# Block 3 of a two-layer kernel: half 0 run three weights ahead of half 1 at the end, with step lists of its own, and the residual behind the steps

## The chip, the core and the metric

The kernel runs on one core of a Trainium2 chip. The metric is the time of one execution in device microseconds, as the median of several runs; less is better.

## The reference

Two layers act on x, of shape (4, 256, 512), in float32. Each has a mixer and a feed-forward part, each behind a layer norm and added to x:

```python
x = x + _L0_attn_ref(_layernorm(x), ...)   # block 1: gated linear attention, 32 heads, chunks of 128
x = x + _L0_ffn_ref(_layernorm(x), ...)    # block 2: router, 8 of 64 expert biases
x = x + _L1_attn_ref(_layernorm(x), ...)   # block 3: state space mixer, 128 heads of 64, 8 groups
x = x + _L1_ffn_ref(_layernorm(x), ...)    # block 4: 16 of 64 rank-16 adapters
```

Block 3 projects x to a gate, to x/B/C (which go through a causal convolution of four taps and a silu) and to time steps; within chunks of 128 positions it multiplies by decays exp(difference of cumulated steps); the result is gated by silu(gate), normalised over each of the 8 groups of 1024 channels, and projected back to 512:

```python
Y = (Y_diag + Y_off).reshape(b, s, H, P) + hs * D[None, None, :, None]
g = y * jax.nn.silu(gate)
gg = g.reshape(b, s, G, INTER // G)
gg = gg * jax.lax.rsqrt(jnp.mean(gg * gg, axis=-1, keepdims=True) + EPS)
return jnp.einsum('bsi,oi->bso', gg.reshape(b, s, INTER) * norm_w, out_proj_w)
```

Block 4 takes the 16 largest of 64 scores per row, their softmax as gates, and adds the gated low-rank products.

## The kernel before

The 1024 rows are two halves of 512 (half 0 and half 1), each of four tiles of 128 rows. x stays in SBUF. Every large projection is done in float32 accuracy by three matmuls of split operands (high times high, high times low, low times high), so one projection of 128 channels (`proj`, L197) is 12 matmuls of 128x512.

Weights come in blocks of 512 KB through the class `Weights`: a DMA from SP's queue into one of two raw buffers (L167), a cast to the high part on ACT (L135), a subtraction for the low part on POOL (L138).

Block 3 (`state_space`) goes over pairs of channel chunks. A pair (g, cp, half) is two chunks of 128 channels of group g (0 to 7), cp from 0 to 3, for one half; it needs three weights: wx (input), wg (gate), wo (output). Its steps, each a letter in a step list:

- I0, I1 (`inputs`): 12 matmuls ps_x; the convolution as one ACT pass and three DVE passes (`conv`, L709); a silu on ACT. G0, G1 (`gate`): 12 matmuls ps_g, silu on ACT.
- X0, X1 (`sums`): a DMA gb of broadcast cumulated steps (L283), their differences on DVE and POOL (m, L290), a causal mask on POOL (L292). D0, D1 (`decays`): exp on ACT (each change between silu and exp is a table load, L1112), then DVE's product with the group's matrix (m, L750).
- T0, T1 (`turn`): transposes, then xd and xe on DVE (L774, L783). M0, M1 (`mixer`): 12 small matmuls ps_y; xs on DVE (L807) and its gate product on POOL (L811); yh on ACT, yl on DVE (L816); a square on ACT whose sum sqs is kept on POOL (L825).
- O0 to O3 (`output`): for each row tile six matmuls ps_o (L851, two PSUM buffers) that DVE adds to acc (L857). In the last pair of a group (cp = 3) step O0 first makes r, the inverse root of the mean square (`scale`: 8 PE records ps_m, one DVE, one POOL instruction, L837), and each O adds its tile to x with `x += acc * r` (L860, the residual).
- B is the group's B and C, W starts one more weight, and P and E take one step of the side work in `k.side` (E also where that step needs an exp table).

One round of the loop in `run` has three pairs: O of `before`, T and M of `p`, all else of `after`. The order of pairs is written out: the first four weights run half 0 and then half 1; then each weight runs both halves in turn; the last `LONE3` weights run half 0 and then half 1 again, and each half loads its own weights. With `LONE3 = 2` the pairs end with

    (7,1,0) (7,1,1) | (7,2,0) (7,3,0) (7,2,1) (7,3,1)

A half that has all its groups goes to `done(half)`, which puts block 4's preparation of that half into `k.side`: statistics (L83), rstd on POOL (L87, L88), xn (L96), transposes, xs_hi and xs_lo (L121, L122), the logits (ps_lg), the 16 largest on DVE, the gates through DRAM and, for half 0, 96 matmuls ps_h (`first`). `adapters.run` then does the rest: hid of half 0, half 1's preparation, 96 output matmuls of half 0 (ps_o, L1077), 96 matmuls ps_h and 96 output matmuls of half 1. The low parts of its weights (wa, wb) are POOL subtractions too.

The step lists are program order. The framework's scheduler then moves instructions of each engine by its own estimate of readiness, so the built order, not the list, is what an engine runs; each engine runs its instructions strictly in that order.

Of the kernel before, what the change touches and what calls it, by code (L numbers as in the profile page):

```python
# [18 lines left out]
P = 128  # L19
# [3 lines left out]
HT = NT // 2  # L23
# [1 line left out]
EPS = 1e-5  # L25
GONE = -30000.0
YB = 3
LONE1, FIRST3, LONE3 = 3, 1, 2
PUMP = 1
AHEAD = 0  # L30
BANK1, BANK3 = "o", "x"
# [1 line left out]
STEP1 = "K S0 W T S1 S2 W G0 G1 K C K P U A0 K W P A1 T P P Q0 N0 W W N1 Q1 T T W K D F".split()  # L33
SIDE1 = "S0 W G0 T P K C W W P P W S1 K G1 S2 U P A0 N0 A1 P Q0 T W T F W N1 K Q1 T T D W W".split()
STEP3 = "W T0 T1 B I0 W M0 M1 X0 X1 I1 O0 G0 W W O1 W W P O2 W W G1 P W O3 D0 D1 W W".split()
FILL3 = "B X0 X1 I0 I1 P P G0 G1 W W P P W D0 D1 E E".split()
SIDE3 = "T0 T1 I0 I1 M0 M1 P B X0 X1 P P O0 W O1 G0 G1 W W P O2 O3 W P W P D0 D1 E E".split()

# [610 lines left out]
def state_space(k, tc, io):  # L649
# [4 lines left out]
    NC = 8  # L654
# [60 lines left out]
    def group(p):  # L715

        g, half = p.g, p.half
        bc = [
            k.wk.tile([P, FREE], F32, tag="y", name=f"bc_{g}_{half}_{n}", bufs=4) for n in range(2)
        ]  # L720
        for n, first in enumerate((BS, CS)):
            conv(proj(k, tc, chunk(p.w.bc(), n), half, f"bc_{g}_{half}_{n}"), bc[n], first + g)
        s = own.only.tile([P, 3, 2, P], F32, tag="cb", name=f"cb_{g}_{half}", bufs=2)
        for b in range(2):
            ps = k.psum.tile([P, 3, P], F32, tag="x", name=f"ps_cb_{g}_{half}_{b}")
            for n, (zs, zl) in enumerate(((0, 0), (1, 1), (0, 1))):
                fs, fl = (2 * b + zs) * P, (2 * b + zl) * P
                nc.tensor.matmul(
                    ps[:, n, :], bc[0][:, fs:fs + P], bc[1][:, fl:fl + P],
                    start=True, stop=True,  # L730
                )
            own.copied = nc.scalar.copy(s[:, :, b, :], ps)
        cbs[g, half] = s

    def sums(p, n):
        hs = slice(2 * (p.ch + n), 2 * (p.ch + n) + 2)
        p.e[n] = exponents(
            k, tc, cum[p.half][:, hs, :], start[p.half][:, :, hs], f"{p.name}_{n}", 2
        )

    def decays(p, n):


        m, across = p.e.pop(n)
        exps = k.act(m[:, 2], across, AF.Exp), k.act(m[:, 0:2], m[:, 0:2], AF.Exp)
        if p is pairs[0]:
            for one in exps:
                k.behind(one, own.copied, "C.B first")
        mh = m.rearrange("p z (h b) l -> p z h (b l)", h=2)
        made = nc.vector.tensor_tensor(  # L750
            mh, mh, cbs[p.g, p.half].rearrange("p z b l -> p z (b l)").unsqueeze(2)
            .to_broadcast([P, 3, 2, 2 * P]), ALU.mult,
        )
        p.m.append(m)
        p.due.append(made)

    def inputs(p, n):
        xs = k.wk.tile([P, FREE], F32, tag="a", name=f"xs_{p.name}_{n}", bufs=4)
        conv(proj(k, tc, chunk(p.w.x(), n), p.half, f"x_{p.name}_{n}"), xs, p.ch + n)
        p.xs.append(xs)  # L760

    def gate(p, n):
        sg = k.wk.tile([P, FREE], F32, tag="sg", name=f"sg_{p.name}_{n}", bufs=4)
        k.act(sg, proj(k, tc, chunk(p.w.g(), n), p.half, f"g_{p.name}_{n}", "g"), AF.Silu)
        p.sg.append(sg)

    def turn(p, n):

        nm, ch, xs = f"{p.name}_{n}", p.ch + n, p.xs[n]
        ps = k.psum.tile([P, HT, P], F32, tag="y", name=f"ps_t_{nm}")  # L770
        for t in range(HT):
            nc.tensor.transpose(ps[:, t, :], xs[:, t * P:t * P + P], k.ident)
        xd = k.wk.tile([P, HT, 2, D], F32, tag="xd", name=f"xd_{nm}")
        made = nc.vector.tensor_tensor(  # L774
            xd, ps.rearrange("p t (h d) -> p t h d", h=2),
            dt[p.half][:, :, 2 * ch:2 * ch + 2].unsqueeze(3)
            .to_broadcast([P, HT, 2, D]), ALU.mult,
        )
        p.xd.append(xd)
        p.due.append(made)  # L780
        if n == 0:
            p.xe = k.wk.tile([P, 2, 2, 2, D], F32, tag="xn", name=f"xe_{p.name}", bufs=1)
        made = nc.vector.tensor_tensor(  # L783
            p.xe[:, n], ps.rearrange("p (b z) (h d) -> p b z h d", b=2, h=2)[:, :, 0],
            start[p.half][:, 2, 2 * ch:2 * ch + 2, :].rearrange("p h b -> p b h").unsqueeze(3)
            .to_broadcast([P, 2, 2, D]), ALU.mult,
        )
        p.due.append(made)
# [38 lines left out]
    def scale(p):  # L827

        ps = k.psum.tile([P, HT], F32, tag="y", name=f"ps_m3_{p.name}")
        for t in range(HT):  # L830
            nc.tensor.matmul(
                ps[:, t:t + 1], sqs[p.g, p.half][:, t * P:t * P + P], k.ones,
                start=True, stop=True,
            )
        p.r = k.small([P, HT], f"r3_{p.name}", "r")
        nc.vector.tensor_scalar(p.r, ps, 1.0 / (NC * P), EPS, ALU.mult, ALU.add)
        nc.gpsimd.tensor_tensor(p.r, p.r, k.neghalf, ALU.pow)  # L837

    def output(p, t):
        if p.cp == 0 and t == 0:  # L840
            acc[p.g, p.half] = k.wk.tile([P, HT, HID], F32, tag="big", name=f"acc_{p.name}")
        if p.cp == NC // 2 - 1 and t == 0:
            scale(p)
        ps = k.psum.tile([P, HID], F32, tag="o", name=f"ps_o3_{p.name}_{t}")
        at = slice(t * P, t * P + P)
        i = 0
        for n in range(2):
            yh, yl = p.y[n]
            wh, wl = p.w.o()
            for y, w in ((yh, wh), (yh, wl), (yl, wh)):  # L850
                nc.tensor.matmul(ps, y[:, at], w[:, n, :], start=(i == 0), stop=(i == 5))  # L851
                i += 1
        a = acc[p.g, p.half][:, t, :]
        if p.cp == 0:
            nc.scalar.copy(a, ps)
        else:
            nc.vector.tensor_tensor(a, a, ps, ALU.add)  # L857
        if p.cp == NC // 2 - 1:
            xt = k.x[HT * p.half + t]
            nc.vector.scalar_tensor_tensor(xt, a, p.r[:, t:t + 1], xt, ALU.mult, ALU.add)  # L860

    cbs, sqs, acc = {}, {}, {}

    pairs, uses = [], []
# [4 lines left out]
    for together in order:  # L869
        pair = [(*divmod(n, NC // 2), half) for half in range(2) for n in together]  # L870
        for g, cp, half in pair:
            p = Ctx()
# [16 lines left out]
    def run(done):  # L889


        with tc.tile_pool(name="s3", bufs=1, reuse_waits="tile") as own.only:
            for i in range(-1, len(pairs) + 1):
                k.bank = BANK3 if i >= 0 else "o"
                before, p, after = (
                    pairs[j] if 0 <= j < len(pairs) else None for j in (i - 1, i, i + 1)
                )
                if i + 2 < len(pairs):
                    k.weights.due = pairs[i + 2].w.g.n
                else:  # L900
                    k.weights.due = len(k.weights.all) - 1
                if after is not None and after.half not in ready:
                    k.pump(1000, True)

                def shared():
                    if after.cp == 0:
                        group(after)

                def put(t):
                    output(before, t)  # L910
                    if t == HT - 1 and all(one.half != before.half for one in pairs[i:]):
                        done(before.half)

                step = dict(
                    B=shared, I=lambda n: inputs(after, n), G=lambda n: gate(after, n),
                    X=lambda n: sums(after, n), D=lambda n: decays(after, n), T=lambda n: turn(p, n), M=lambda n: mixer(p, n),
                    O=put, W=k.weights.step, P=k.pump, E=lambda: k.pump(1, True),
                )
                for one in FILL3 if i < 0 else SIDE3 if k.side else STEP3:
                    who = {"T": p, "M": p, "O": before, "P": k, "E": k, "W": k}.get(one[0], after)  # L920
                    if who is not None and (i >= 0 or not AHEAD or one[0] not in "IG"):
                        step[one[0]](*(int(n) for n in one[1:]))

    def ahead(i):

        p = pairs[0]
        assert 0 in ready
        n = i % 2
        if i < 2:
            inputs(p, n)  # L930
        elif i < 4:
            gate(p, n)
        else:
            sums(p, n)
# [315 lines left out]
```

## Time and profile before

| what | value |
|---|---|
| median of 3 runs (lowest, highest) | 2555.05 us (2549.81, 2555.57) |
| profiled execution: time; span | 2553.7 us; 2551.9 us |
| mean granted TensorE clock | 0.987 |
| PE, DVE, ACT, POOL busy | 96%, 80%, 57%, 62% of the span |
| first ps_g of pair (7,1,1) | 2301.1 us |
| table loads ahead of the exps of (7,1,0), (7,1,1), (7,2,0), (7,3,0), (7,2,1) | 2308.34, 2328.06, 2346.46, 2366.81, 2388.30 us |
| first matmul of half 1's last output tile | 2542.2 us |

PE is TensorE, DVE VectorE, ACT ScalarE, POOL GpSimd, SP SyncE. Times are microseconds from the start of the span. A number such as L857 is a line of the kernel before. Busy time is the time in which an engine had an instruction at work; a matmul of 128x512 lasts about 0.39 and the next starts 0.227 after it. "[6.61 <-DVE acc L857]" means that the engine was idle for 6.61 before this instruction, and that DVE's instruction on line 857 ended that.

### The profile page before, as it was taken

The page shows a single profiled execution, that of the slowest core. Times are in us where ns is not written, and L with a number is a line of the kernel's source. Part 1 is how long each engine was busy: PE and PEld are TensorE (multiplying, and loading weights), DVE is VectorE, ACT ScalarE, POOL GpSimd, SP SyncE. Part 2 cuts the span into 40 slices and gives each one's busy share as a digit, 9 for nine tenths or more (in the row PEclk, how much of TensorE's full clock was granted, in tenths as well). Part 3 has the DMA queues.
Part 4 walks back from the last instruction along what each step waited for, and adds up shares of the span by engine and source line. Part 5 has one row for each costly group of instructions (what it writes and reads, how often), then busy time and mean ns, then how long its engine had stood idle before and what let it go on. Part 6 is the DMA issues. An engine that isn't in the chain of part 4 may idle for free.

```text
span 2551.9 us, 36913 instructions
## 1 busy us (share of the span) xinstructions
PE 2438.3 (96%) x14000; PEld 2012.3 (79%) x14000; DVE 2037.0 (80%) x2629; ACT 1453.8 (57%) x2363; POOL 1584.7 (62%) x1123
## 2 busy tenths in 40 slices
PE   7999999999999998899999999999999999999899
PEld 6788787888877876678878888888888888887677
DVE  6776676767777878697998988988988988979873
ACT  3554454545554555475765756666757657657631
POOL 4655445556575646586774875856756865857840
PEclk9999999999999998999999999999999999999999
DMA  3321212212221322242322323322323223323321
GB/s 107 85 71 48 54 44 63 70 58 83 83 91 56 97 73 85 73 128 73 97 91 67 97 78 88 92 70 91 99 68 100 84 67 96 100 62 108 93 77 68
DMA packets 82896, 206.25 MB, mean 81 GB/s; under 512 B 8672, under 2 KB 10592, under 8 KB 82720
## 3 DMA queue, kind: packets, MB, share of 16 engines
q1 hardware_dynamic: 82720, 203.90, 26.6%
q8 instruction: 111, 1.82, 0.3%
q14 instruction: 65, 0.53, 0.1%
HBM read 200.86 MB, written 3.01 MB: 80 GB/s over the span
## 4 chain that ended last, share of the span: by engine, by line
PE 59%; DVE 17%; POOL 10%; ACT 6%; issue 5%; DMA 2%; SPq 0%; POOLq 0%; ACTq 0%; DVEq 0%
PE ps_g L197 12%; PE ps_x L197 8%; PE ps_o L851 8%; PE ps_o L452 5%; PE ps_q L197 5%; DVE m L750 4%; PE ps_y L797 4%; DVE conv L709 3%; PE ps_bc L197 3%; PE ps_sc L396 2%; PE ps_y L408 2%; POOL m L290 2%; ACT L1112 2%; POOL xs L811 2%; DVE yl L816 2%
## 5 line engine op out<-in xcount | busy, mean ns | idle before, releaser
L197 PE MATMUL ps_g<-xs_hi,wg_h 128*128 128x512 f32 x768 | 305.7, 398 | 5.3 <-ACT wg_h L135 2.4
L750 DVE TENSOR_TENSOR m<-m,cb 128x1536 f32<-128x1536 f32 x128 | 274.1, 2145 | 41.3 <-ACT m L1115 40.2
L197 PE MATMUL ps_g<-xs_lo,wg_h 128*128 128x512 f32 x768 | 300.9, 392 | 0.0
L197 PE MATMUL ps_g<-xs_hi,wg_l 128*128 128x512 f32 x768 | 299.6, 393 | 0.0
L709 DVE SCALAR_TENSOR_TENSOR conv<-ps_x,cw,conv 128x510 f32<-128x510 f32 (+2 forms) x384 | 269.9, 736 | 21.9 <-ACT conv L707 19.1
L1112 ACT ACT_TABLE_LOAD x191 | 245.1, 1283 | 3.8 <-PEq L1238 0.8
L851 PE MATMUL ps_o<-wo_h,yh 128*128 128x512 f32 x512 | 212.5, 415 | 19.4 <-DVE acc L857 18.6
L290 POOL TENSOR_TENSOR m<-gb,start 128x512 f32<-128x512 f32 x128 | 150.5, 1178 | 127.6 <-PE ps_y L797 82.1
L811 POOL TENSOR_TENSOR xs<-xs,sg 128x512 f32<-128x512 f32 x128 | 207.8, 1624 | 29.4 <-DVE xs L807 28.5
L825 POOL TENSOR_TENSOR sqs<-sqs,sq 128x512 f32<-128x512 f32 x112 | 193.3, 1726 | 34.6 <-ACT sq L823 34.2
L138 POOL TENSOR_TENSOR wo_l<-raw_wo,wo_h 128x1024 fp32r<-128x1024 f32 x60 | 148.1, 2468 | 93.2 <-ACT wo_h L135 87.4
L851 PE MATMUL ps_o<-wo_h,yl 128*128 128x512 f32 x512 | 199.3, 403 | 5.9 <-DVE yl L816 5.9
L197 PE MATMUL ps_x<-xs_lo,wx_h 128*128 128x512 f32 x512 | 203.0, 396 | 0.0
L851 PE MATMUL ps_o<-wo_l,yh 128*128 128x512 f32 x512 | 202.7, 396 | 0.0
L197 PE MATMUL ps_x<-xs_hi,wx_h 128*128 128x512 f32 x512 | 202.4, 395 | 0.0
L197 PE MATMUL ps_x<-xs_hi,wx_l 128*128 128x512 f32 x512 | 201.6, 394 | 0.0
L292 POOL TENSOR_SCALAR_AFFINE_SELECT m<-m 128x1024 f32<-128x1024 f32 x160 | 200.5, 1253 | 0.1
L1115 ACT ACTIVATE xs<-conv,cb 128x512 f32<-128x512 f32 x128 | 90.8, 723 | 191.5 <-DVE conv L709 191.5
L138 POOL TENSOR_TENSOR wx_l<-raw_wx,wx_h 128x1024 fp32r<-128x1024 f32 x38 | 96.1, 2529 | 159.8 <-ACT wx_h L135 147.1
L797 PE MATMUL ps_y<-m,xd 128*64 128x128 f32 x2048 | 177.7, 279 | 10.9 <-DVE m L750 8.1
L1115 ACT ACTIVATE m<-m 128x1024 f32<-128x1024 f32 (+1 forms) x160 | 181.6, 1135 | 9.1 <-POOL m L292 8.8
L138 POOL TENSOR_TENSOR wg_l<-raw_wg,wg_h 128x1024 fp32r<-128x1024 f32 x60 | 152.4, 2540 | 50.7 <-ACT wg_h L135 50.7
(276 smaller groups left out, 6894.0 us busy)
## 6 DMA issues: line engine op xcount, KB each, us to landing
gb<-cum SPq DMA_DIRECT2D x160, 512.0 KB
raw_wx<-in_L_attn_in_x_dram SPq DMA_DIRECT2D x38, 512.0 KB
raw_wg<-in_L_attn_in_gate_dram SPq DMA_DIRECT2D x38, 512.0 KB
raw_wo<-n_L_attn_out_proj_w_dram SPq DMA_DIRECT2D x38, 512.0 KB
raw_wq<-in_L_attn_Wq_dram SPq DMA_DIRECT2D x22, 512.0 KB
raw_wg<-in_L_attn_Wg_dram SPq DMA_DIRECT2D x22, 512.0 KB
raw_wo<-in_L_attn_Wo_dram SPq DMA_DIRECT2D x22, 512.0 KB
raw_wkv<-in_L_kv_dram SPq DMA_DIRECT2D x11, 512.0 KB
```

The costliest lines, as they stand in the source:

```text
L138: nc.gpsimd.tensor_tensor(lo, w, hi.bitcast(F32), ALU.subtract)
L197: tc.nc.tensor.matmul(ps, a[:, c, :], b[:, c, :], start=(c == 0 and n == 0), stop=(c == KC - 1 and n == 2))
L290: engine.tensor_tensor(m[:, blk], gb[:, min(blk, 1)], last(at, P), ALU.add)
L292: nc.gpsimd.affine_select(out=causal, in_=causal, compare_op=ALU.is_ge, fill=GONE, base=0, pattern=[[0, 8], [1, P]], channel_multiplier=-1,)
L709: nc.vector.scalar_tensor_tensor(acc[:, :, j:], ps[:, :, :SEQ - j], cw[:, ch, TAPS - 1 - j:TAPS - j], acc[:, :, j:], ALU.mult, ALU.add,)
L750: made = nc.vector.tensor_tensor(mh, mh, cbs[p.g, p.half].rearrange("p z b l -> p z (b l)").unsqueeze(2) .to_broadcast([P, 3, 2, 2 * P]), ...
L797: one = nc.tensor.matmul(ps_y[h * D:h * D + D, 2 * b + z, :], p.xe[:, n, b, h, :] if blk == 2 else xd[:, 2 * b + zs, h, :], m[:, blk, 2 * ...
L811: nc.gpsimd.tensor_tensor(xs, xs, p.sg[n], ALU.mult)
L825: nc.gpsimd.tensor_tensor(total, total, sq, ALU.add)
L851: nc.tensor.matmul(ps, y[:, at], w[:, n, :], start=(i == 0), stop=(i == 5))
L1112: load = nc.scalar.preload_act_table_set(table)
L1115: ins = nc.scalar.activation(out, in_, func, bias=bias, scale=scale)
```

## The change

`LONE3` becomes 3. The pairs end with

    (7,1,0) (7,2,0) (7,3,0) (7,1,1) (7,2,1) (7,3,1)

so (7,1) loads its three weights twice, and half 0 is complete one pair earlier. The last three rounds of the loop take their steps from `LAST3`; there the side steps P and E stand between the steps of the pair. The residual of a group leaves `output` and runs for all four tiles behind all steps of the round, and `done(half)` after it.

```diff
-LONE1, FIRST3, LONE3 = 3, 1, 2
+LONE1, FIRST3, LONE3 = 3, 1, 3
...
+LAST3 = [one.split() for one in (
+    "T0 T1 P I0 M0 M1 P X0 X1 I1 P O0 G0 W O1 G1 P O2 P O3 D0 D1 W P W",
+    "T0 T1 E M0 M1 E W O0 E O1 W E O2 E O3 E",
+    "E O0 W E O1 E O2 E O3 E",
+)]
...
-        if p.cp == NC // 2 - 1:
-            xt = k.x[HT * p.half + t]
+
+    def residual(p):
+
+        for t in range(HT):
+            xt, a = k.x[HT * p.half + t], acc[p.g, p.half][:, t, :]
             nc.vector.scalar_tensor_tensor(xt, a, p.r[:, t:t + 1], xt, ALU.mult, ALU.add)
...
+                left = i - (len(pairs) - 2)
...
-                def put(t):
-                    output(before, t)
-                    if t == HT - 1 and all(one.half != before.half for one in pairs[i:]):
-                        done(before.half)
-
...
-                    O=put, W=k.weights.step, P=k.pump, E=lambda: k.pump(1, True),
+                    O=lambda t: output(before, t), W=k.weights.step, P=k.pump, E=lambda: k.pump(1, True),
                 )
-                for one in FILL3 if i < 0 else SIDE3 if k.side else STEP3:
+                for one in FILL3 if i < 0 else LAST3[left] if left >= 0 else SIDE3 if k.side else STEP3:
...
+                if before is not None and before.cp == NC // 2 - 1:
+                    residual(before)
+                    if all(one.half != before.half for one in pairs[max(i, 0):]):
+                        done(before.half)
```

In the built program PE's order stays as it was up to the first ps_g of (7,1,1); SP, ACT and POOL part some 20 us earlier, in the order of the weight loads alone. The number of matmuls is the same.

## The prediction

> **What bounds the kernel now.** I read first the page, then the built order of both kernels against each other, then the trace from the place where they part. The page has PE at 96% of the span, so only time in which PE does not work can be won. PE's two orders are equal up to the gate projections of pair (7,1,1), half 1 of the last weights that before runs for both halves in turn; the trace puts those at 2301.1 us. (SP, ACT and POOL part at 2279 to 2292, where weights change places: wo of (7,1) later, wg of (7,2) earlier, in times in which POOL sat idle.) Both programs have equally many matmuls. So the question is the last 251 us, and in it PE's idle and slow time. Busy time by stretch there (core 0: stretch, length, then busy us and instructions of each engine, granted clock, DMA share, GB/s):
>
> ```profile
> core 0: us, PE busy (x) PEld busy (x) DVE busy (x) ACT busy (x) POOL busy (x), PEclk, DMA share, GB/s
> ...
> 2330.00:2350.00 20.00, 20.00 (x130) 16.65 (x129) 18.46 (x24) 16.51 (x23) 14.23 (x11) 1.00 0.31 84
> 2350.00:2370.00 20.00, 18.61 (x121) 15.03 (x120) 19.85 (x23) 13.35 (x18) 19.13 (x11) 1.00 0.42 128
> 2370.00:2391.00 21.00, 19.64 (x125) 15.90 (x124) 19.50 (x21) 13.19 (x18) 21.00 (x12) 1.00 0.45 126
> 2391.00:2417.00 26.00, 20.35 (x132) 16.50 (x130) 20.07 (x23) 15.05 (x21) 21.02 (x13) 0.99 0.27 81
> 2417.00:2443.00 26.00, 19.42 (x97) 14.83 (x98) 25.56 (x34) 11.78 (x18) 23.13 (x18) 0.61 0.27 86
> 2443.00:2475.00 32.00, 31.62 (x154) 25.72 (x152) 20.32 (x59) 8.81 (x16) 11.62 (x13) 1.00 0.20 62
> 2475.00:2500.00 25.00, 22.37 (x98) 17.47 (x98) 16.68 (x49) 7.06 (x12) 2.40 (x1) 1.00 0.21 74
> ```
>
> Up to 2350 PE is full. In 2350 to 2391, where each pair brings three weights of its own, POOL is full (40.1 of 41) and DVE nearly (39.4), and PE loses 2.75. In 2391 to 2443 PE loses 12.2 and runs at clock 0.61, while DVE is full. After 2443 PE is the bound again. The waits of PE in 2301 to 2476 name the places (total, times, longest):
>
> ```profile
> PE ps_o L851 <- DVE acc L857: 7.7, 3, 6.6
> PE ps_y L797 <- DVE m L750: 4.7, 3, 3.0
> PE ps_y L797 <- POOL rstd L87: 1.7, 1, 1.7
> ```
>
> The 6.6 stands at 2411. DVE's timeline tells why: the last accumulation of half 0's group, whose PSUM buffer PE needs, is queued behind three residuals, and these behind a wait of 5.39 for POOL's r.
>
> ```profile
> 2407.06 0.69 DVE L857 TENSOR_TENSOR acc<-acc,ps_o 128x512 f32<-128x512 f32 x1
> 2413.14 4.17 DVE L860 SCALAR_TENSOR_TENSOR x<-acc,r,x 128x512 f32<-128x512 f32 x3 [5.39 <-POOL r L837]
> 2417.24 0.68 DVE L857 TENSOR_TENSOR acc<-acc,ps_o 128x512 f32<-128x512 f32 x1
> ```
>
> POOL's timeline shows what r waits for: a weight of the adapter (wa_l), then the gate product, the causal mask, the sum of squares.
>
> ```profile
> 2405.64 2.96 POOL L138 TENSOR_TENSOR wa_l<-raw_wa,wa_h 128x1024 fp32r<-128x1024 f32 x1
> 2408.55 1.29 POOL L811 TENSOR_TENSOR xs<-xs,sg 128x512 f32<-128x512 f32 x1
> 2409.79 1.09 POOL L292 TENSOR_SCALAR_AFFINE_SELECT m<-m 128x1024 f32<-128x1024 f32 x1
> 2410.85 1.27 POOL L825 TENSOR_TENSOR sqs<-sqs,sq 128x512 f32<-128x512 f32 x1
> 2412.08 1.02 POOL L837 TENSOR_TENSOR r<-r,neghalf 128x4 f32<-128x4 f32 x1
> ```
>
> **The change part by part.** The profiled execution took 2553.7 us (span 2551.9); the median of the runs is 2555.05, so I add 1.35 at the end. One step of 0.3% is 7.7 us, about what a measurement of this kernel can tell from no change.
>
> (a) Three more weights. Pair (7,1) no longer shares wx, wg, wo between its halves: three DMAs of 512 KB, three ACT casts of 1.04 and three POOL subtractions of 2.4 (wg_l median 2.41; up to 3.91 when they collide with DVE). SP's queue: a weight lands 3.5 after issue and gb pairs 6 to 7, on DMA engines at 0.27 to 0.45; the order issues each weight one POOL subtraction ahead of need, so I cost the DMAs at nothing; if that cover is gone, a pair waits up to 3.5. ACT has 26 us free of 90 in 2301 to 2391: nothing. POOL is the case. From 2301 to half 0's r it was busy 95.4; the new order has one pair's work less before that r (two gate products of 1.74, two masks of 1.1, two sums of 1.3, two m of 1.04: 10.4) and one subtraction more (2.4): 87.4. So r can't come before 2388.7, and POOL is as full as in 2350 to 2391. There two pair steps cost PE 2.75; in 2301 to 2350, with shared weights, nothing. Two more steps now run in that manner: 2.75 late. Bounds: 0 (PE is full at 20 per pair anyway) to 7.2 (three subtractions of 2.4 wholly on the path).
>
> The page "SBUF — State Buffer", section "Who interferes with whom" of the Trainium skill, speaks against the change: a DVE instruction with two SBUF inputs and a POOL instruction that reads SBUF lock each other out for a whole instruction. The rows: DVE's product m L750 takes 1.72 at least and 3.36 at most in 2290 to 2430. By the rule three subtractions could hold DVE for 7.2, by the rows for 3 x 1.64 = 4.9; the sum below does without either.
>
> (b) The residual behind the pair's steps. In the built order all four accumulations of (7,3,0) now stand ahead of the four residuals, and PE has then 24 input and 12 gate matmuls of (7,3,1) in its queue (36 x 0.227 = 8.2). So the 6.61 stall goes. What is late next: DVE still waits for r, and behind the residuals stand the products of (7,2,1), for which y of that pair waits. In before r was done 12.4 after DVE's first xs of the pair; wa_l (2.96) is no longer ahead of it, so the wait is 5.39 - 2.96 = 2.4 (bounds 0 and 5.4).
>
> (c) DVE's path, from the end of the products before ((7,3,0) at 2376.0; in the new order (7,1,1), so 2378.8 with (a)). To the residuals: one yl 1.2, six conv of 0.66, two xs of 0.65, two m L290 of 1.0, four acc of 0.6, one yl 0.7, r 0.1 = 11.7, so 2390.5; wait 2.4; three residuals 3.0 (0.7 alone, 1.39 each in the row above); xd and xe 1.9; two products 4.4; residual 1.0; two statistics 1.2. Products of (7,2,1) done at 2404.4, against 2395.8 before. PE, unhindered, reaches that y's end at 2403 (before's 2398.6 and 20 matmuls more), so it waits about 3 there.
>
> Then, to the last pair's products, the adapter's preparation of half 0 now stands in front: two statistics 1.2, four aggregates 0.4, three yl 2.2, six conv 4.0, two xs 1.3, two m 2.0, eight acc 4.8, xd and xe 1.9, four xn 3.4 (0.55 alone, up to 2.26), three xs_lo 1.9 = 23.1. The exponents need silu 0.72, table 1.28, exp 0.63 and 1.04 behind the last conv, 3.7, with 1.9 of DVE work beside them: 1.8 more. Products 4.0, last xs_lo 0.65. Half 0's logits can run from 2404.4 + 29.6 = 2434.0.
>
> In before the body of those logits starts at 2443.45, with 455 matmul rows left; the new order has 470 left there. 15 x 0.227 = 3.4: gain 2443.45 - 3.4 - 2434.0 = 6.0.
>
> (d) The clock. The row of 2417 to 2443 has 0.61: after the 6.6 stall a matmul starts every 0.43 instead of 0.227. PE waits for DVE in that stretch, so only y of the last pair, 2.7 against 1.4 each, is on the path; this is within (c). "TensorE: Matmul & The Clock Gate", "Seeing it yourself", shows, in one run of its own, a throttle 5.2 after the last matmul; by it the new waits of 1 to 4 would leave the clock up, but PE waits for DVE either way.
>
> (e) The tail. From half 1's last transposition 312 rows in the same order follow in both. Its rstd now stands on POOL behind a wb subtraction (2.39): 3.0 late. Against that gT of half 0 moves up by about 11, so that the 2.6 idle in 2475 to 2500 (hid of half 0 late) goes, 2.5. Bounds -3 to +3.
>
> Sum: -6.0 + 3.0 - 2.5 = -5.5. Execution 2548.2, median 2549.5.
>
> **Rivals.** Faster, 0.36: DVE's contended ops at their lone lengths. Residuals 2.1, products 3.4 twice, m 1.3, xn 2.2, no wait for r, nothing for (a): 2.75 + 2.4 + 0.9 + 1.6 + 0.7 + 1.2 = 9.6 more, 2540. For it: PE full to 2350; against it: DVE was full in 2350 to 2391 and 2417 to 2443 with just these collisions.
>
> Slower, 0.13: POOL becomes the bound. If the three subtractions take their collided 3.91 on the path (11.7 instead of 2.75) and r keeps its wait of 5.4, half 0's logits start at 2446, the tail's rstd is still late, and the end is 6.5 to 8 behind before: 2562. It decides once POOL's gate products lag DVE's xs by more than about 8; in before the lag is at most 6.
>
> No gain, within the middle case (0.51): DVE's work after 2301 is the same in sum, 20 us of it idle; if what the 6.6 stall frees comes back as waits for y and for xn, the end moves by less than 2.
>
> **How the numbers follow.** The middle case, -7.7 to +7.7 around a gain of 5.5, has 0.51; its own range is 2547 to 2557. Faster by over 0.3% 0.36, slower 0.13. Low 2540 is the faster rival's end, high 2561 just inside the slower one's. All bounds of (a) to (e) at once would give 2538 to 2565.
>
> **What would show it.** Right: no wait of ps_o for acc above 2 near 2405; clock 1.0 or near in 2400 to 2440; y's wait for m in two places, 3 and more; half 0's logits at about 2434. Wrong: POOL over 97% from 2301 on and a wait of DVE for r above 5 (slower), or logits before 2428 (faster); a changed time before 2301 would overturn the premise.

## The result, and the profile after

The changed kernel takes 2572.07 us (median, 2570.23 to 2574.55) beside 2555.31 for the kernel before (2549.81 to 2556.28): a ratio of 1.007, 95% interval 1.0058 to 1.0082. It is 16.8 slower, 0.7%, and the interval is clear of 1. The forecast was 2549.5 in 2540 to 2561, so direction and range were both wrong. The profiled execution has a span of 2572.7 (clock 0.983) against 2551.9 (0.987).

The two traces can be laid over each other up to 2301, where PE's orders part. There the run after is already 2.9 late, on equal instructions. That lies within the spread between executions: a build whose order equals before's on every engine (e10 below) stood 2.5 late at 2280. All trace times below are as printed; where traces are compared, each run's lateness ahead of 2301 is taken off (2.9 here), and the text says "corrected".

In rows of the changed kernel and of versions built on it, line numbers are its own, in block 3 six higher than before: ps_o is L857, acc L863, the products m L756.

The first view is busy time by stretch, as in the prediction (length, then busy us and instructions of each engine, granted clock, DMA share, GB/s):

```profile
core 0: us, PE busy (x) PEld busy (x) DVE busy (x) ACT busy (x) POOL busy (x), PEclk, DMA share, GB/s
2330.00:2350.00 20.00, 19.21 (x123) 15.38 (x122) 16.19 (x17) 18.43 (x26) 17.05 (x11) 1.00 0.42 128
2350.00:2370.00 20.00, 14.95 (x96) 12.18 (x96) 19.93 (x22) 10.70 (x15) 17.21 (x11) 0.93 0.39 106
2370.00:2391.00 21.00, 21.00 (x131) 17.35 (x131) 19.98 (x20) 12.80 (x16) 19.98 (x12) 0.98 0.39 126
2391.00:2417.00 26.00, 24.10 (x147) 19.40 (x146) 24.13 (x34) 14.23 (x19) 21.68 (x17) 1.00 0.31 88
2417.00:2443.00 26.00, 16.03 (x54) 11.05 (x52) 20.63 (x25) 8.19 (x13) 18.67 (x16) 0.79 0.19 60
2443.00:2475.00 32.00, 25.92 (x141) 20.66 (x142) 18.32 (x46) 14.80 (x21) 14.49 (x9) 0.80 0.21 66
2475.00:2500.00 25.00, 18.85 (x85) 15.42 (x84) 17.29 (x31) 8.19 (x14) 6.80 (x10) 0.87 0.18 59
```

There are three losses. PE is idle 5.8 in 2330 to 2370 (1.4 before); from 2417 to 2475 it is idle 16 (7 before) although neither DVE nor POOL is full there; and 6.2 in 2475 to 2500 (2.6 before). In 2391 to 2417 it gains 3.8. PE's waits in 2301 to 2500 (total, times, longest):

```profile
PE ps_y L803 <- DVE m L756: 9.6, 4, 4.1
PE ps_o L857 <- DVE acc L863: 7.5, 4, 3.5
PE ps_xn L110 <- DVE xs_lo L128: 7.1, 2, 4.8
PE ps_xn L110 <- DVE conv L715: 2.6, 1, 2.6
```

The 6.6 for acc near 2411 is gone, as forecast, though PE's waits for acc come to 7.5 in all where they were 7.7: 6.3 of it now stands in 2420 to 2443. DVE's timeline shows the residuals behind all four accumulations, with a wait of 1.55 for r where 5.39 stood:

```profile
2398.44 0.69 DVE L863 TENSOR_TENSOR acc<-acc,ps_o 128x512 f32<-128x512 f32 x1 [0.33 <-PE ps_o L857]
2400.67 2.08 DVE L869 SCALAR_TENSOR_TENSOR x<-acc,r,x 128x512 f32<-128x512 f32 x3 [1.55 <-POOL r L843]
```

What no step of the prediction has is in ACT's timeline. The first tap of a convolution (L713) is ACT's; the last pair (7,3,1) has two, one for each input chunk:

```profile
2403.66 0.68 ACT L713 ACTIVATE conv<-ps_x,cw 128x512 f32<-128x512 f32 x1
...
2429.44 0.58 ACT L127 CAST xs_hi<-ps_xn 128x512 fp32r<-128x512 f32 x1 [1.74 <-PE ps_xn L110]
2429.92 0.63 ACT L829 ACTIVATE sq<-xs 128x512 f32<-128x512 f32 x1
2439.90 0.69 ACT L713 ACTIVATE conv<-ps_x,cw 128x512 f32<-128x512 f32 x1 [9.35 <-PE ps_xn L110]
```

The second tap runs 36 after the first (in before they are back to back, at 2396), and it waits not for its input (PE's last matmul of it starts at 2404.26) but for transpositions of half 0's normalised tiles. It writes a tile of tag `cv`, which has two buffers, and the normalisation for the adapters is called with `("xn", "cv", "cv")`: its second and third tile in flight take the same two. In the first own list two P stand ahead of I1, so the normalisation is asked for the buffers first. The second tap must then wait until xn_4_1 is made by DVE (the pair of xn at 2430.52 to 2433.5) and transposed by PE (2439.26):

```profile
2430.52 3.03 DVE L102 TENSOR_SCALAR xn<-x,mv,rstd 128x512 f32<-128x512 f32 x2
...
2439.26 0.60 PE L110 MATMUL ps_xn<-ident,xn 128*128 128x128 f32 x4
...
2451.01 0.70 PE L803 MATMUL ps_y<-m,xd 128*64 128x128 f32 x4 [3.56 <-DVE m L756]
```

The last row is the first y of the last pair. Behind the tap stand the convolution, the exponents, the last pair's products and its y.

### The profile page after: what moved, and what is told of

Same layout as the page of the kernel before. It is cut to its first block, busy times and chain, and to the rows that moved or that the text cites. A ratio compares the mean times of both kernels' runs of the same rounds, so it can differ in the third digit from the quotient of the medians.

```text
span 2572.7 us, 36943 instructions
## 1 busy us (share of the span) xinstructions
PE 2446.0 (95%) x14000; PEld 2017.9 (78%) x14000; DVE 2045.9 (80%) x2629; ACT 1457.2 (57%) x2366; POOL 1588.7 (62%) x1126
## 5 line engine op out<-in xcount | busy, mean ns | idle before, releaser
L756 DVE TENSOR_TENSOR m<-m,cb 128x1536 f32<-128x1536 f32 x128 | 274.2, 2147 | 37.2 <-ACT m L1124 36.0
L857 PE MATMUL ps_o<-wo_h,yh 128*128 128x512 f32 x512 | 212.4, 415 | 19.7 <-DVE acc L863 18.2
L144 POOL TENSOR_TENSOR wo_l<-raw_wo,wo_h 128x1024 fp32r<-128x1024 f32 x61 | 151.9, 2490 | 98.2 <-ACT wo_h L141 92.4
L857 PE MATMUL ps_o<-wo_h,yl 128*128 128x512 f32 x512 | 199.8, 403 | 8.1 <-DVE yl L822 8.1
L857 PE MATMUL ps_o<-wo_l,yh 128*128 128x512 f32 x512 | 202.6, 396 | 0.0
L822 DVE SCALAR_TENSOR_TENSOR yl<-xs,nw,yh 128x512 fp32r<-128x512 f32 x128 | 170.4, 1331 | 24.5 <-ACT yh L821 24.5
L144 POOL TENSOR_TENSOR wg_l<-raw_wg,wg_h 128x1024 fp32r<-128x1024 f32 x61 | 157.6, 2583 | 51.2 <-ACT wg_h L141 51.2
```

The source lines that it names most:

```text
L144: nc.gpsimd.tensor_tensor(lo, w, hi.bitcast(F32), ALU.subtract)
L756: made = nc.vector.tensor_tensor(mh, mh, cbs[p.g, p.half].rearrange("p z b l -> p z (b l)").unsqueeze(2) .to_broadcast([P, 3, 2, 2 * P]), ...
L822: nc.vector.scalar_tensor_tensor(yl, xs, w, yh.bitcast(F32), ALU.mult, ALU.subtract)
```

## The experiments

All runs stand beside runs of before made on the same chip (medians of 2554.8 to 2555.2); a ratio is to those, with its 95% interval.

**1. Buffers of tag cv.** Two runs take that wait away, each in its own manner. e1 moves one step in the first own list:

```
-"T0 T1 P I0 M0 M1 P X0 X1 I1 P O0 G0 ...
+"T0 T1 P I0 M0 M1 X0 X1 I1 P P O0 G0 ...
```

> The changed kernel with one step moved: in the first of the own lists, I1 (input of the last pair's second chunk) stands ahead of the two P steps in which half 0's normalisation takes both buffers of tag cv. Theory (cv buffers): in the changed kernel the first tap of that chunk, conv_159, waited on ACT until 2439.90 for the buffer that xn_4_1 held, and the last pair's y started at 2451; with I1 first the tap runs right behind conv_158 (2404), that y at about 2436, half 0's logits at about 2441 instead of 2456.7, and the time is 2572 - 15 = 2557 (2553 to 2562). Rival (three more weights: POOL and DVE full of subtractions and products): the order of two steps changes neither, 2570 to 2574. Rival (PSUM bank x shared by ps_x and ps_xn): the order of allocation changes here too, so it expects a gain as well, 2557.

Measured 2562.69, ratio 1.003 (1.002 to 1.004). e2 leaves the list and changes the buffers:

```
-yield from normalize(k, tc, half, "4", ("xn", "cv", "cv"))
+yield from normalize(k, tc, half, "4", ("xn", "y", "y"))
```

> The changed kernel with only the buffers of the normalisation for the adapters changed: its second and third tile in flight take buffers of tag y (four, of which half 0's are free by then) instead of the two of tag cv; the step lists and PSUM banks stay. Theory (cv buffers): conv_159 no longer waits for xn_4_1; y of the last pair at about 2436, time 2557 (2553 to 2562). Rival (PSUM bank x): the program's order of ps_x and ps_xn is unchanged, the same chain stays, 2570 to 2574. Rival (three more weights): 2570 to 2574.

Measured 2560.15, ratio 1.0023 (1.0014 to 1.0031). ACT's timeline of e2 has both taps in one row:

```profile
2401.07 1.26 ACT L713 ACTIVATE conv<-ps_x,cw 128x512 f32<-128x512 f32 x2
```

e1 lands 0.7 above its range, e2 inside. The rival of PSUM bank x is out, since e2 leaves the banks as they are; so is the rival that the three weights hold the whole loss. With everything else as in the changed kernel, the buffers cost 9.4 (e1) to 11.9 (e2). But 5 to 8 stay.

**2. Lists and lead apart.** e3 drops the own lists from the changed kernel; e4 makes only half 0's lead of three weights, in before.

```
-for one in FILL3 if i < 0 else LAST3[left] if left >= 0 else SIDE3 if k.side else STEP3:
+for one in FILL3 if i < 0 else SIDE3 if k.side else STEP3:      # e3

-LONE1, FIRST3, LONE3 = 3, 1, 2
+LONE1, FIRST3, LONE3 = 3, 1, 3                                  # e4
```

> The changed kernel without its own step lists: the last three rounds use the lists of before (half 0 three weights ahead and the residual behind the steps stay). Theory (cv buffers): the old list for rounds with side work has I0 and I1 ahead of its first P, so conv_159 follows conv_158 at once, and the time is 2550 to 2560. Rival (three more weights): nothing changes on POOL and DVE ahead of the last pair, 2570 to 2574.

Measured 2570.56, ratio 1.0055 (1.0041 to 1.0068).

> Before with one part of the change alone: half 0 runs the last three weights ahead of half 1 (three instead of two); step lists and residual as before. Theory (cv buffers): no wait for a cv buffer, so this is before plus what three unshared weights cost, less what half 0's earlier end gives: 2550 to 2560, as the run without own lists. Rival (three more weights): it holds the whole loss, 2570 to 2574.

Measured 2571.4, ratio 1.0062 (1.0049 to 1.0075). Both missed: the time came out where the rival of the three weights expected it, but e7 below shows that the weights do not cost that much. Their second tap does follow the first, but in PE's built order the last pair's y stands behind half 0's logits and three adapter chunks. It starts at 2457 and 2454 (2424 before), and half 1's tiles for the adapters then come one by one: in e4 PE waits 9.1 for them in three waits (2479 to 2490), and its work in 2475 to 2500 is 13.8 of 25. So the lead costs some 16 with the old lists too. That the next cause does it there is read from the two traces; no run tests it.

**3. Half 1's last outputs.** The tail of e1, PE first and then DVE:

```profile
2476.45 1.03 PE L110 MATMUL ps_xn<-ident,xn 128*128 128x128 f32 x8
2483.02 1.12 PE L110 MATMUL ps_xn<-ident,xn 128*128 128x128 f32 x4 [5.54 <-DVE xs_lo L128]
2485.45 1.09 PE L110 MATMUL ps_xn<-ident,xn 128*128 128x128 f32 x4 [1.31 <-DVE xn L102]
```

```profile
2477.78 0.69 DVE L1065 TENSOR_TENSOR gate<-gate,raw 128x512 f32<-128x512 f32 x1 [2.26 <-DMA gate<-gates]
2478.39 0.68 DVE L863 TENSOR_TENSOR acc<-acc,ps_o 128x512 f32<-128x512 f32 x1
```

The last sum of half 1 follows its output projection, which stands behind chunk 6 of half 0's adapters, and on DVE it queues behind a gate product of half 0 that waits 2.26 for a DMA. When half 1's chain (sum, residual, statistics, centred tile, transposition) begins, half 0's eight chunks are nearly used up, and PE has nothing to put beside it. In before the last output is at 2458 with four and a half chunks still to come. e5 (on e1) and e6 (on the changed kernel) put half 1's outputs ahead:

```
-"T0 T1 E M0 M1 E W O0 E O1 W E O2 E O3 E",      # e5 alone
+"T0 T1 M0 M1 W O0 E O1 W E O2 E O3 E",
-"E O0 W E O1 E O2 E O3 E",                      # e5 and e6
+"O0 W O1 O2 O3 E E E E E",
```

> The run with I1 first, and half 1's last pair also no longer interleaved with half 0's adapter: the last own list becomes O0 W O1 O2 O3 E E E E E, and the one before it loses its first two E. Theory (two causes): with I1 first the time was 2562.7, and its profile still shows PE waiting 5.8 and 1.7 for half 1's normalised tiles, since the last two output projections of half 1 stood behind h4_0_5 and h4_0_6 and half 0's rows were used up by then; with the outputs first half 0's h4 rows lie beside that chain, 6 less: 2556.5 (2552 to 2561). Rival (cv buffers and three weights are all): the tail's wait moves elsewhere, 2561 to 2564.

Measured 2556.73, ratio 1.0009 (1.0000 to 1.0017): 6.0 off e1, as expected to 0.2 (the two waits in the rows above are 5.54 and 1.31, a little less than the expectation has them), and at most 0.2% above before.

> The changed kernel with only the last own list altered, O0 W O1 O2 O3 E E E E E in place of E O0 W E O1 E O2 E O3 E: the wait for a buffer of tag cv stays. Theory (two causes that add): 6 less than the changed kernel, 2566 (2562 to 2569). Rival (cv alone holds the loss and the tail's wait is its echo): 2570 to 2573.

Measured 2570.0, ratio 1.0065 (1.0053 to 1.0077): 2.1 off. That is the lower edge of the rival's range and above the theory's, and the intervals of the two ratios overlap. So the losses do not simply add: the last list alone gives at most some 2 here. It gave 6.0 in e5, where the wait for cv is gone and the list before it has lost two E as well; no run separates these two. While the cv wait stays, the last pair is late itself and its outputs end at 2481.7, with three chunks left.

**4. Three weights alone.** e7 is before with (7,1) loaded twice:

```
-if pairs and (pairs[-1].g, pairs[-1].cp) == (g, cp):
+if pairs and (pairs[-1].g, pairs[-1].cp) == (g, cp) and (g, cp) != (7, 1):
```

> Before, with wx, wg and wo of pair (7,1) loaded, cast and split a second time for half 1 instead of being shared; order of pairs, lists and residual as before. Theory: the weights cost the 4.4 of PE that all runs with half 0 three ahead lose more than before in 2330 to 2370, wholly or in part: 2557 to 2560. Rival (they hold most of the loss): 2568 and more. Rival (DVE's later waits hide them): 2555.

Measured 2561.45, ratio 1.0029 (1.0018 to 1.0040): 6.3 slower, 1.5 above the theory's range and far from the rival's 2568. Busy time by stretch and PE's waits in 2301 to 2391 of e7:

```profile
2350.00:2370.00 20.00, 15.01 (x97) 12.09 (x95) 19.93 (x22) 10.78 (x16) 17.20 (x11) 0.90 0.39 106
```

```profile
PE ps_y L797 <- DVE m L750: 4.9, 2, 4.1
```

This is the changed kernel's row almost to the digit: the products of the third pair in a row that brings weights of its own come 4.1 late, with DVE full. These 4.1 are the greater part of the 6.3; behind 2475 PE also waits 3.6 for half 1's xs_lo ahead of its logits (0.7 before), and what makes that was not followed.

**5. Lists and residual without the lead; residual alone.** e8 is the changed kernel with `LONE3` back at 2. e10 is before with the residual written behind the steps of the pair (the diff's `residual` and `done`), and nothing else.

> The changed kernel with half 0 only two weights ahead, as in before: own step lists and the residual behind the steps stay. Theory (cv buffers): half 0's residual then ends within the round of the first own list, so its normalisation cannot take cv ahead of I1, and (7,1) shares its weights: 2551 to 2559. Rival (lists or residual cost by themselves): 2562 and more.

Measured 2561.3, ratio 1.0028 (1.0018 to 1.0038): it misses the theory's range by 2 and falls short of the rival's. Its profile has PE waiting 8.6 for acc at 2412 (6.6 before) and 4.1 for half 1's xs_lo near 2476. Which of the two parts does it was not pursued beyond e10, which speaks for the lists. A wait of 4 for half 1's xs_lo behind 2475 thus comes without the lead too (4.1 here, 4.0 in e13 below).

> Before with one part of the change alone: the residual and the end of a half written behind the steps of the pair; half 0 two weights ahead and the old lists. The scheduler leaves DVE's order as in before (three residuals ahead of the last acc), so the 6.6 stall stays. Theory (this part does nothing by itself): 2554 to 2557. Rival (the place in the program decides): the stall goes, 2549 to 2551.

Measured 2555.51, ratio 1.0004 (0.9994 to 1.0014). The built program equals before in the order on every engine: this part of the change does nothing by itself. In its trace the longest wait for acc in 2301 to 2476 is 5.5. In e4, which has the lead alone, it is 2.8. So the lead, not the residual's place in the source, removed the 6.6 stall.

**6. Is the 6.6 stall on the path?** e9 and e13 tie the residuals behind the last accumulation on DVE, e9 in all sixteen groups, e13 for half 0's last alone:

```
+one = nc.vector.scalar_tensor_tensor(xt, a, p.r[:, t:t + 1], xt, ALU.mult, ALU.add)
+if p.g == 7 and p.half == 0:                    # e13 alone
+    k.behind(one, own.added, "residual behind the last sum")
```

> Before, with the four residuals of a group tied behind the group's last accumulation by an order on DVE; order of pairs, weights and lists as before. The built order has the last acc ahead of the residuals here, so the wait of PE for its PSUM buffer, 6.6 at 2411, should go. Theory A (DVE sets that stretch; PE's stall only passes the time until the last pair's products): half 0's logits and the end stay, 2553 to 2557. Theory B (the prediction's first step: the stall is on the path): 2549 to 2551.

Measured 2574.19, ratio 1.0074 (1.0062 to 1.0087). It answers nothing on the question: the tie cost 14 ahead of 2286, in the other groups.

> Before, with the four residuals tied behind the last accumulation for half 0's last group alone (the run that tied them in all sixteen had lost 14 by 2286, ahead of the place in question). Theory A (DVE sets the stretch; the 6.6 stall only passes the time until the last pair's products): half 0's logits at 2442 to 2445 as in before, time 2553 to 2558. Theory B (the stall is on the path): logits at about 2438, 2549 to 2551.

Measured 2560.6, ratio 1.0024 (1.0014 to 1.0033). PE's waits in 2301 to 2476:

```profile
PE ps_o L851 <- ACT yh L815: 6.5, 2, 5.6
PE ps_y L797 <- DVE m L750: 5.6, 4, 3.0
PE ps_o L851 <- DVE acc L857: 2.3, 3, 0.8
```

The 6.6 for acc is gone and one of 5.6 for ACT's yh stands in its place: PE is idle from about 2414 to 2419.9, and the last pair's y starts at 2425.0 as before (2424.4). Half 0's logits are at 2444.9, the upper edge of theory A. So the stall only passed time until the last pair's y. The total is 3 above A's range; its built tail has half 1's logits ahead of half 0's outputs, and PE waits 4.0 for xs_lo there.

**7. Does DVE set 2417 to 2443?** e11 and e12 are e5 with half 0's four centred tiles made by ACT; e12 writes the bias over the variance instead of into a new small tile. e14 is e5 with six small tiles allocated and never used.

```
-tc.nc.vector.tensor_scalar(xn, k.x[t], *of, ALU.subtract, ALU.mult)      # e11 and e12, half 0 only
+nb = k.small([P, 1], f"nb_{t}", "ln_nb", 6)               # e11 and e14; e12: nb is mv[:, 1:2]
+tc.nc.gpsimd.tensor_tensor(nb, mean, rstd, ALU.mult)      # e11 and e12, half 0 only
+tc.nc.gpsimd.tensor_scalar_mul(nb, nb, -1.0)
+tc.nc.scalar.activation(xn, k.x[t], AF.Identity, scale=rstd, bias=nb)
```

> The run with I1 and half 1's outputs first (2556.7), and half 0's four centred tiles for the adapters made by ACT (scale rstd, bias minus mean times rstd, two small ops on POOL each) instead of DVE. In that run DVE is busy 25 of 26 in 2417 to 2443 while ACT has 14.6; the four took DVE 0.55 to 2.3 each. Theory (DVE sets that stretch): 3 to 5 less, 2552 to 2554, below before. Rival (POOL, 24.8 of 26 there, or the chain of half 0's transposes sets it): 2556 to 2559.

Measured 2569.76, ratio 1.0059 (1.0045 to 1.0072), a miss on both sides; 13 of it had come by 2280, ahead of any instruction that differs.

> As the run with ACT making half 0's centred tiles, but minus mean times rstd is written over the variance, so that no tile is added to the pool of small tiles. That run was 13 late, and 13 of it had come by 2280, in steps of about half a microsecond per 100, ahead of any instruction that differs. Theory (DVE sets 2417 to 2443): with the small tiles where they were, 3 to 5 less than 2556.7, so 2552 to 2554. Rival (POOL, or the chain of half 0's transposes): 2556 to 2559. Rival (ACT's new instructions cause the early loss, through code or tables): 2568 to 2571.

Measured 2559.37, ratio 1.0021 (1.0011 to 1.0030): no gain. The stretch in e5, then in e12:

```profile
2417.00:2443.00 26.00, 15.85 (x98) 12.24 (x100) 24.99 (x31) 14.61 (x21) 24.76 (x17) 0.93 0.26 77
```

```profile
2417.00:2443.00 26.00, 15.09 (x58) 10.63 (x56) 19.07 (x24) 16.30 (x22) 25.69 (x25) 0.80 0.22 69
```

DVE lost 5.9 of work and PE did no more: POOL, at 24.8, went to 25.7 and the last pair's y from 2440.9 to 2446.8. DVE and POOL were both full there, and taking work off DVE alone won nothing. Whether POOL or the chain of half 0's transpositions held it then was not separated.

> The run with I1 and half 1's outputs first (2556.7), and six unused tiles of 4 bytes a partition added to the pool of small tiles; the order on every engine is equal in both. Theory (the place of tiles in SBUF costs the 13 that came before 2280 in the run with ACT's centred tiles): 2567 to 2571, spread evenly over the span. Rival (that run's own instructions): 2555 to 2559.

Measured 2567.53, ratio 1.0051 (1.0037 to 1.0065): the layout theory, see the last section. e11's 13 has the same cause as far as the traces tell.

No version beat the kernel before; e5, with three losses cut to one, comes level.

## Why the prediction was wrong

Its terms, corrected times, against what was measured:

| step | predicted | measured |
|---|---|---|
| (a) three weights | 2.75 late (0 to 7.2) | 6.3 (e7) |
| (b) stall of 6.6 | goes; r-wait 2.4 | goes; r-wait 1.55; worth nothing (e13) |
| (c) products of (7,2,1) done | 2404.4 | 2409.2 |
| (c) half 0's logits | 2434.0 | 2453.8; without the cv wait 2443.0 (e1), 2441.5 (e5) |
| (e) tail | 0.5 late | 6.0 late (e1 to e5) |

**The step that failed** is (c), in the sentence that sums the work "to the last pair's products". It lists DVE's operations with their durations and lets the exponents follow "behind the last conv", but takes for granted that the last conv can start. The prediction put that wait at nothing, because it did not follow the buffers: the own list asks for two `cv` tiles for the normalisation ahead of I1, and the second tap, ready near 2405, waits until 2439.9. Taking that wait away gives 9.4 of the 16.8 (e1), or 11.9 (e2). The built order of ACT has the tap behind the normalisation's first cast; the prediction went through PE, DVE and POOL, and costed ACT only as free time. Ahead of that, the path of (c) was 4.8 late at the products of (7,2,1); 3.3 of it stood already at those of (7,1,1), which ended at 2382.1 corrected: 6.1 after the 2376.0 of before, where (a) had allowed 2.75.

One row was also misread in the opening: "in 2391 to 2443 ... DVE is full" at clock 0.61 holds for 2417 to 2443 alone (DVE 25.56 of 26). In 2391 to 2417 DVE has 20.07 of 26, with the 5.39 for r in it, and the clock is 0.99.

**Mis-sized: (a).** The value taken was what two such pairs had cost before; the same weights one pair earlier cost 6.3 (e7), near the upper bound, 4.1 of it in one wait for the products. The rule of the Trainium skill ("SBUF — State Buffer", "Who interferes with whom") that spoke against the change put it at 7.2, the rows at 4.9, and the sum went without either. In the changed kernel's trace one of two that overlap is long each time: a subtraction of 2.40 at 2336 with DVE's product at 3.22, one of 3.90 at 2342 with the product at 1.75. Those rows fit the rule, though no run separates the lock from full queues.

**Mis-sized: (e).** Rstd behind a wb subtraction was seen and costed at 3.0, and the gate products' DMA at 2.5 the other way. What moved was larger: half 1's last outputs fall behind half 0's adapter chunks, which were the cover of half 1's chain. Putting the outputs ahead gave 6.0 once the buffers were free (e1 to e5), and at most some 2 for the last list alone before that (e6). "312 rows in the same order follow" holds from the last transposition on (75.3 to the end, 77.5 before); the loss lies just ahead of it.

**Held, and worth nothing: (b).** The stall went and the r-wait shrank, yet e13 shows the same 6 passing as a wait for yh. The prediction had named this itself, as "No gain" within its middle case: what the stall frees comes back as other waits. If the weights cost 6.3 in the new order too, which no run shows, the order itself gained 6.3 - 1.6 = 4.7 (e5 is 1.6 above before), against 8.25 in the prediction (5.5 and 2.75). That the terms -4.7, 6.3, 9.4 and 6.0 then add up to about the 16.8 is no check: they are differences of the same four times, so they must.

**Wrong: (d), without weight in the sum.** Clock was to stay near 1.0 with waits of 1 to 4. It was 0.79 and 0.80 in 2417 to 2475, with no single wait above 3.6 there. The clock fell to half four times between 2367 and 2456, behind or within waits of 2.3 to 4.1 (last section). The section of the Trainium skill that the prediction used shows one event 5.2 after the last matmul, which is an example and no threshold; the page's rule stands in "What's actually happening" of "TensorE: Matmul & The Clock Gate": half clock after one idle window of about 3.4, in windows that run freely. The trace agrees on two points: it took no 5.2, and the stretches at half clock last 3.41 or a multiple of it. It does not show that a window must be idle: in the 3.41 ahead of three of the four falls PE had worked 1.0 to 1.4 (last section). Here the measurement decides.

**The rival on the slower side** named POOL and 2562. The sign was right and e7's 6.3 is part of its price, but POOL was not the bound where most was lost: it worked 18.7 of 26 in 2417 to 2443, and DVE waited 1.55 for r, not 5.4.

## What to carry to other kernels

When steps of two streams are re-ordered, follow each tag's buffers in the order in which the program asks for them, not only the engines' queues: an early request of one stream can hold a later step of the other although its input has long been there. Before moving work of one half ahead, see what it was covering; the last chain of the other half may have had nothing else. A stall of PE is worth what the next wait lets through: here 6.6 were removed and came back as another name.

## What was not expected of the hardware

**Place of tiles in SBUF.** e14 and e5 have equal instructions in equal order on every engine; e14 only moves tiles, by six small ones. It is 10.8 slower (0.4%), and the loss is spread evenly: from 300 to 2280 the steps between matmul starts that lie in 215 to 240 ns, some 5,860, have a mean of 230.3 ns in e14 and e11 and 228.4 in e5, e12, before and the others. 5,860 x 1.9 ns is 11.1. PE's idle time in that stretch did not grow (68.6 in e5, 62.7 in e14). Why that place costs 0.8% of the time from start to start was not found, but a difference of 0.4% between two versions can come from where their tiles lie. The comparisons above between versions with 228.4 do not show this effect.

**The clock after a short wait.** In the changed kernel PE waits 4.08 for the products at 2367, then runs at 0.72 for the next 6, and at 1.00 after that:

```profile
2361.00:2367.00 6.00, 1.92 (x27) 1.35 (x26) 6.00 (x4) 3.27 (x6) 5.79 (x3) 1.00 0.29 87
2367.00:2373.00 6.00, 5.99 (x37) 5.06 (x38) 5.93 (x9) 1.90 (x3) 6.00 (x4) 0.72 0.28 89
2373.00:2379.00 6.00, 6.00 (x32) 4.99 (x31) 4.98 (x8) 5.92 (x8) 6.00 (x6) 1.00 0.13 41
```

So a wait of 4 here costs more than its 4: the matmuls behind it start at about half the rate for some 3.4. In this trace the clock between 2367 and 2456 falls to 0.50 four times, for 3.41, 3.41, 6.83 and 13.65. Three of the four, each with the 3.41 ahead of the fall and then the stretch at half clock:

```profile
2363.90:2367.31 3.41, 0.30 (x6) 0.33 (x8) 3.41 (x3) 0.37 (x1) 3.41 (x2) 1.00 0.50 154
2367.31:2370.72 3.41, 3.41 (x26) 2.88 (x23) 3.34 (x6) 0.72 (x1) 3.41 (x3) 0.50 0.15 22
...
2428.75:2432.16 3.41, 1.39 (x7) 0.65 (x5) 3.41 (x2) 1.11 (x2) 3.41 (x2) 1.00 0.31 76
2432.16:2438.99 6.83, 4.79 (x11) 3.80 (x12) 3.87 (x6) 0.00 (x0) 2.60 (x3) 0.50 0.35 116
2438.99:2442.40 3.41, 1.16 (x9) 0.81 (x8) 2.47 (x4) 2.11 (x3) 0.32 (x1) 1.00 0.00 0
2442.40:2456.05 13.65, 7.52 (x46) 5.66 (x44) 9.79 (x11) 8.13 (x11) 6.47 (x3) 0.50 0.14 41
```

Ahead of the four falls PE had worked 0.30, 1.00, 1.39 and 1.16 of 3.41. The third came 0.8 after PE's last matmul had ended, within a wait of 2.81. So several waits of 1 to 3 close together, with little work between them, took the clock down here as one of 4 did.
